# Values of two quads in one run from quad 44 on, in a fused cross-attention kernel

## The chip, the core and the metric

The kernel runs on one core of one Trainium2 chip. The metric is the time of one execution on the device in microseconds (us). Engines are named as in the profile: PE is TensorE (matmuls; PEld its weight loads), DVE VectorE, ACT ScalarE, POOL GpSimd, SP SyncE, whose queue issues nearly all transfers. Each engine works through its own list of instructions in order; semaphores tie the lists together.

## The reference

Eight batches of 256 tokens attend to 256 context rows each, with 32 heads of 32 columns. Keys and values are the context itself. All data are float32.

```python
x_ = (x - mu) * rsqrt(var + 1e-5) * ln_gamma + ln_beta      # (8, 256, 1024)
Q = split_heads(x_ @ Wq.T); K = V = split_heads(ctx)         # 32 heads x 32
scores = where(mask, einsum('bhsd,bhtd->bhst', Q, K) / sqrt(32), -inf)
probs = softmax(scores)
out = x + merge_heads(einsum('bhst,bhtd->bhsd', probs, V)) @ Wout.T
```

## The kernel before

**Quads and slots.** Four heads (128 columns) are a quad; eight batches of eight quads give 64. The main loop has a slot for each quad n, and the program's order is each engine's order (the schedule is manual). In slot n PE gets, in this order: the scores of quad n + 1 (line 493), output-projection steps of "place 0", the values of quad n - 2 (line 643), steps of "place 1", one eighth of a later batch's query projection (line 216, `pq`), and steps of "place 2". The softmax of quad n + 1 goes to the other engines in the same slot.

**Softmax** (`softmax_parts`), head by head of the quad: DVE adds the mask and takes the row minimum of the negated scores out of PSUM (line 531), ACT exponentiates and sums the row (535), DVE takes reciprocals (542), POOL scales (550), DVE transposes 32 x 32 blocks into the tile `pT` (556). ACT sets one half of `pT` aside (562), and SP's queue exchanges halves between partitions by four transfers (621, 625). Then PE can form the values. From quad 57 on the last transposes and the transfers (`tail`) are put off to the next quad's softmax. The first exponentials of a quad are followed, on ACT, by the copies of finished values: `copy_at` (line 656) takes the two PSUM banks of a quad, `pv` for r = 0 and 1, into the tile `at`, with one chunk for each quad and one tile for each half batch.

**Buffers.** `pT` has three buffers, tag `pv` two PSUM banks, the scores (`sc`) four, `pq` and `po` one each. The pool `xp` has two buffers, each of the size of a `pT`. They hold a batch's x and its transposed blocks `xe` in turn; the last batch's x is used up in slot 44, and its `xe` by transfers soon after. In slot 60 one buffer takes x again for the final sum (`x_again`).

**Projections.** The output projection of a batch is a 2 x 2 block product with seven products (Strassen-Winograd; `PRODUCTS`) of four steps each, one step for each chunk (quad) of the operand: A11 with quads 0 to 3, A12 with 4 to 7, then S2, S3, A22, S1, S4. The sums S1 to S4 are made by POOL (line 703). The 28 steps of batch b are spread over the slots 8(b + 1) to 8(b + 1) + 8 by a table with a triple for each slot, the number of steps at places 0, 1 and 2. The seventh batch has its own table, `ENDS`: its results are copied off the bank `po` by ACT (`copy_po`, line 745) and added by POOL. For the others DVE reads the bank: `take` (765) and `store` (769). A product that begins the bank anew, or adds to it, must wait for these readers. From slot 59 on a step of the last batch (`po_last`) stands at each slot's end. After the loop come the last batch's remaining products, `po_end` and `po_last`, between the values of quads 62 and 63.

**Order around the change.** The lists are written out by the loop; the transfers stand on SP's queue where a softmax issues them. A load of v for two quads is issued at the end of a softmax and waits until the buffer's last values are formed.

## Time and profile before

| | us |
|---|---|
| median of 3 executions (562.49 to 563.6) | 563.45 |
| the profiled execution, whole | 562.29 |
| its span (first to last instruction) | 560.5 |
| PE busy | 555.1 (99%) |
| DVE busy | 466.3 (83%) |
| ACT busy | 423.7 (76%) |
| POOL busy | 392.9 (70%) |

A row of a timeline gives the start, the time from the first start to the last end, the engine, the line, the tiles written and read, and how many instructions are merged; what stands in brackets is the engine's idle time before the row and what ended it. Runs on PE overlap at their ends, so what a run costs is the distance from its start to the next run's start. One matmul of float32 in the program is two in the profile: 32 rows of the lists below are x64 in a timeline. The slots 48 to 63 start with the scores at 416.50, 424.02, 432.34, 440.72, 449.96, 458.34, 466.73, 475.11, 483.49, 492.73, 499.33, 505.94, 512.54, 519.15 and 525.75, and slot 63, which has no scores, with values at 532.35.

### The profile page before, as it was taken

How to read it: one execution, taken by the hardware profiler on the slowest of the kernel's cores; microseconds unless marked ns; L12 is line 12 of the kernel's file. 1: busy time of each engine (PE TensorE's matmuls, PEld its weight loads, DVE VectorE, ACT ScalarE, POOL GpSimd, SP SyncE). 2: the span in 40 equal slices, each digit the busy share in tenths (PEclk: the TensorE clock that was granted, in tenths of full speed). 3: DMA queues.
4: the chain of work that ended last, by engine and by line, in shares of the span. 5: the costliest groups of instructions: out<-in, count | busy, mean ns of one | idle time of the engine just before them, and what ended most of it. 6: DMA issues, size and time to landing. Idle time of an engine off the chain costs nothing.

```text
span 560.5 us, 24339 instructions
## 1 busy us (share of the span) xinstructions
PE 555.1 (99%) x9334; PEld 357.0 (64%) x9334; DVE 466.3 (83%) x1716; ACT 423.7 (76%) x1464; POOL 392.9 (70%) x635
## 2 busy tenths in 40 slices
PE   8999999999999999999999999999999999999997
PEld 7666665767656767567765676566766766744443
DVE  5979889999998888988898888988888878879823
ACT  3699999998769867797777877778776876869920
POOL 1688887999797666867568666777648657448780
PEclk9999999999999999999999999999999999999999
DMA  8967657957678767877778767788667874536752
GB/s 305 397 188 209 184 150 235 319 179 223 207 253 246 246 183 223 259 204 232 217 232 233 207 186 233 221 233 239 176 166 249 244 228 130 149 91 182 209 169 76
DMA packets 47236, 119.30 MB, mean 213 GB/s; under 512 B 8976, under 2 KB 9744, under 8 KB 47120
## 3 DMA queue, kind: packets, MB, share of 16 engines
q1 hardware_dynamic: 46832, 117.48, 69.5%
q8 instruction: 74, 1.21, 1.0%
q14 instruction: 42, 0.34, 0.2%
q10 hardware_dynamic: 288, 0.27, 0.1%
HBM read 66.33 MB, written 11.53 MB: 139 GB/s over the span
## 4 chain that ended last, share of the span: by engine, by line
PE 98%; DVE 1%; DMA 1%; ACT 0%; POOL 0%; issue 0%; POOLq 0%
PE po_S L216 20%; PE pq_A L216 19%; PE pv L643 12%; PE sc L493 12%; PE po_A L216 11%; PE pq L216 10%; PE pq_S L216 7%; PE po_end L216 3%; PE po_last L216 1%; DMA x<-in_x_dram 1%; PE po_end_s L216 0%; PE px L280 0%; PE px L314 0%; ACT e L535 0%; DVE st L234 0%; DVE xnT L289 0%
## 5 line engine op out<-in xcount | busy, mean ns | idle before, releaser
L550 POOL TENSOR_SCALAR e<-e,rden 128x256 f32<-128x256 f32 x466 | 215.5, 479 | 124.2 <-DVE rden L542 121.7
L535 ACT ACTIVATE e<-e,mn 128x256 f32<-128x256 f32 x512 | 254.0, 501 | 43.6 <-DVE mn L531 43.1
L556 DVE STREAM_TRANSPOSE pT<-e 128x512 f32<-128x512 f32 x256 | 178.9, 703 | 36.6 <-POOL e L550 27.5
L531 DVE CUSTOM_DVE_ANT_0 e<-sc,mb 128x256 f32<-128x256 f32 x512 | 185.3, 416 | 23.8 <-PE sc L493 23.3
L562 ACT COPY pc<-pT 128x512 f32<-128x512 f32 x128 | 78.9, 616 | 52.2 <-DVE pT L556 34.5
L535 ACT ACTIVATION_READ_ACCUMULATOR e<-e,mn 128x1 f32 x512 | 98.2, 192 | 0.0
L493 PEld LDWEIGHTS sc<-k,qa 32*128 32x128 f32 x1024 | 46.1, 184 | 45.6 <-issue 22.4
L643 PE MATMUL pv<-pT,v 64*32 64x128 f32 x4096 | 74.2, 274 | 0.0
L493 PE MATMUL sc<-k,qa 32*128 32x256 f32 x1024 | 73.6, 400 | 0.2 <-ACT qa L301 0.2
L216 PE MATMUL po_S<-wo,at 128*64 128x512 f32 x304 | 73.5, 598 | 0.0
L643 PEld LDWEIGHTS pv<-pT,v 64*32 64x32 f32 x4096 | 57.1, 105 | 22.7 <-issue 9.6
L216 PE MATMUL po_A<-wo,at 128*64 128x512 f32 x256 | 58.6, 598 | 0.0
L216 PE MATMUL pq<-xnT,wq 128*64 128x256 f32 (+3 forms) x544 | 58.4, 369 | 0.0
L216 PEld LDWEIGHTS pq_A<-xnT,wq 128*64 128x64 f32 x832 | 46.3, 137 | 7.4 <-issue 6.3
L216 PE MATMUL po_S<-wo,s 128*64 128x512 f32 x208 | 49.5, 598 | 0.0
L216 PEld LDWEIGHTS pq<-xnT,wq 128*64 128x64 f32 x544 | 36.8, 136 | 18.9 <-issue 1.8
L216 PE MATMUL pq_A<-xnT,wq 128*64 128x128 f32 x832 | 47.6, 273 | 0.0
L542 DVE RECIPROCAL rden<-den 128x2 f32<-128x2 f32 x256 | 38.3, 150 | 5.8 <-ACT e L535 4.9
L531 DVE DVE_READ_ACCUMULATOR2_ANT mn<- 128x1 f32 x512 | 42.6, 83 | 0.0
L216 PEld LDWEIGHTS po_A<-wo,at 128*64 128x64 f32 x256 | 16.9, 136 | 30.0 <-issue 29.1
L216 PEld LDWEIGHTS po_S<-wo,at 128*64 128x64 f32 x304 | 19.3, 136 | 22.6 <-issue 22.6
L656 ACT COPY at<-pv 128x128 f32<-128x128 f32 x128 | 26.2, 254 | 8.7 <-PE pv L643 8.7
(99 smaller groups left out, 645.4 us busy)
## 6 DMA issues: line engine op xcount, KB each, us to landing
v<-in_kv_dram SPq DMA_DIRECT2D x32, 512.0 KB, 4.8
pT<-pT SPq DMA_DIRECT2D x128, 128.0 KB, 3.3
pT<-pc SPq DMA_DIRECT2D x128, 128.0 KB, 4.1
ring<-kept_T SPq DMA_DIRECT2D x20, 512.0 KB, 5.3
k<-in_kv_dram SPq DMA_DIRECT2D x32, 256.0 KB, 4.0
x<-in_x_dram SPq DMA_DIRECT2D x15, 512.0 KB, 6.6
r<-in_x_dram SPq DMA_DIRECT2D x28, 256.0 KB, 5.1
out_dram<-r SPq DMA_DIRECT2D x28, 256.0 KB, 2.6
```

The source lines that it names most:

```text
L216: nc.tensor.matmul(out[ts(w, P // 2)], stationary[:, ts(w, P // 2)], moving, **flags)
L493: nc.tensor.matmul(scs[n][j][:, s, :], qa[r, n % NQ, ts(s, P)], ks[n - n % 2][r, n % 2, :], start=True, stop=True,)
L531: nc.vector.tensor_tensor_reduce(out=e[:, s, :], in0=pss[j][:, s, :], in1=mbs[n // NQ], scale=1.0, scalar=NO_SCORE, op0=ALU.add, op1=ALU.m ...
L535: nc.scalar.activation(e[:, s, :], e[:, s, :], AF.Exp, bias=mn[:, s : s + 1], scale=-1.0, accum_out=den[:, s : s + 1],)
L542: nc.vector.reciprocal(rden, dens[j])
L550: engine.tensor_scalar(es[j][:, s, :], es[j][:, s, :], rden[:, s : s + 1], 1.0, ALU.mult, ALU.mult,)
L556: nc.vector.transpose(pT[:, :, :, j, :, :].rearrange("p a i s k -> p (a i) s k"), es[j].rearrange("p s (b t) -> p b s t", t=K),)
L562: nc.scalar.copy(pc[:, :, ts(j, 2)], pT[:, 1, :, ts(j, 2)])
L643: nc.tensor.matmul(pvs[n][r][j * HD : (j + 1) * HD], vs[n - n % 2][ts(r, 2 * K), i, ds(n % 2 * P + j * HD, HD)], pT[ts(r, 2 * K), :, i, j, ...
L656: nc.scalar.copy(ats[b, k][:, c, :, ts(r, 2), :], pv.rearrange("p a s k -> p s a k"))
```

## The change

From quad 44 to quad 61 the values of an even quad wait for the odd one behind it: in odd slots PE forms both in one run, in even slots none. Both quads share the two banks, at different columns. After the pair ACT copies four pieces instead of two. An even quad's `pT` is held a slot longer, so a fourth buffer is needed: every fourth quad from 47 on uses one tile out of the pool `xp`. The sixth batch (b = 5) gets a table of its own, since its last quads come in pairs; in slot 49 six steps follow the values instead of seven. The seventh batch's S2 sum is cut into halves instead of three chunks and one.

```diff
+        if n not in SPARE:
+            pTs[n] = ptp.tile([P, 2, NI, NH, NS, K], F32, tag="pT", name=f"pT_{n}")
+        else:
+            if n == SPARE[0]:
+                spare.append(xp.tile([P, 2, NI, NH, NS, K], F32, tag="x", name="pT_spare"))
+            pTs[n] = spare[0]
...
+    PAIRED = range(44, N - 2)
+    SPARE = range(47, N, 4)
+    def due(n):
+        if n - 2 not in PAIRED:
+            return (n - 2,)
+        return (n - 3, n - 2) if n % 2 else ()
...
-    def values(n):
-        pvs[n] = [
-            ps_v.tile([P, 2, NS, K], F32, tag="pv", name=f"pv_{n}_{r}") for r in range(2)
-        ]
+    def values(*quads):
+        if not quads:
+            return
+        banks = [
+            ps_v.tile([P, len(quads), 2, NS, K], F32, tag="pv", name=f"pv_{quads[0]}_{r}")
+            for r in range(2)
+        ]
+        for u, n in enumerate(quads):
+            pvs[n] = [bank[:, u] for bank in banks]
...
     STEPS = ((0, 0, 0), (0, 7, 0), (0, 1, 2), (0, 2, 2), (0, 2, 1), (0, 1, 2), (0, 0, 3), (0, 1, 2),
              (0, 2, 0))
+    STEPS_PAIRED = ((0, 0, 0), (0, 6, 0), (0, 2, 2), (0, 2, 1), (0, 3, 1), (0, 0, 3), (0, 0, 4),
+                    (0, 0, 1), (0, 3, 0))
...
         if n >= 2:
-            values(n - 2)
+            values(*due(n))
...
-            copy_at(n - 2)
+            for done in due(n):
+                copy_at(done)
...
-            sum_at(b, "S2", *((slice(NK - 1, NK),) if b == B - 2 else ()))
+            sum_at(b, "S2", *((slice(NK // 2, NK),) if b == B - 2 else ()))
...
-                sum_at(b, "S2", slice(0, NK - 1))
+                sum_at(b, "S2", slice(0, NK // 2))
```

Where this moves instructions is seen in three places. The first is PE's slot 54, between the scores of quad 55 and the S1 steps of the sixth batch (`po_5_S1`, which begins the bank again); `pq_7_A11` is the query product of the slot. Before, and then after the change:

```order
L493 MATMUL sc_55_3_8603<-k_54_8131,qa_143 128x256
L643 MATMUL pv_52_0_8612<-pT_52_8225,v_52_8286 32x128 [waits DMAHW4_49,DMAHW7_49,DMAHW2_49,Activation_49]
...
L216 MATMUL pq_7_A11_8350<-sx_145,ring_105 64x128 [waits DMAHW1_49,DVE_49,Pool_49]
...
L216 MATMUL po_5_S1_8744<-wo_149,s2_5_7981 64x512 [waits DVE_49,PE_49]
L216 MATMUL po_5_S1_8744<-wo_149,s2_5_7981 64x512 x5
...
L643 MATMUL pv_53_0_8764<-pT_53_8383,v_52_8286 32x128 [waits DMAHW6_49,DMAHW3_49,Activation_49]
```

```order
L493 MATMUL sc_55_3_8594<-k_54_8089,qa_143 128x256
L216 MATMUL pq_7_A11_8309<-sx_145,ring_105 64x128 [waits DMAHW1_49,DVE_49,Pool_49]
...
L216 MATMUL po_5_S1_8697<-wo_149,s2_5_7975 64x512 [waits DVE_49,PE_49]
L216 MATMUL po_5_S1_8697<-wo_149,s2_5_7975 64x512 x7
...
L665 MATMUL pv_52_0_8719<-pT_52_8215,v_52_8279 32x128 [waits DMAHW7_49,DMAHW4_49,Activation_49]
...
L665 MATMUL pv_52_0_8719<-pT_53_8342,v_52_8279 32x128 [waits DMAHW6_49,DMAHW3_49]
```

The values of quad 52 have left the slot and stand ahead of quad 53's in slot 55, in one bank; the steps, now eight rows instead of six, still wait for DVE.

The second is PE's slot 60, with the A22 steps of the seventh batch (`po_6_A11` is the bank's name, `at_6_1` the operand), which wait for ACT's `copy_po` of that bank. Before, and after:

```order
L493 MATMUL sc_61_3_9415<-k_60_9106,qa_143 128x256
L643 MATMUL pv_58_0_9424<-pT_58_9093,v_58_9226 32x128 [waits DMAHW3_49,DMAHW7_49,DMAHW1_49,Activation_49]
...
L216 MATMUL po_6_A11_9040<-wo_149,at_6_1_8687 64x512 [waits Activation_49]
L216 MATMUL po_6_A11_9040<-wo_149,at_6_1_8687 64x512 x7
L216 MATMUL po_last_9408<-wo_149,at_7_0_9232 64x512 x2
L493 MATMUL sc_62_0_9532<-k_62_9349,qa_143 128x256 [waits DMAHW7_49,DVE_49]
```

```order
L493 MATMUL sc_61_3_9398<-k_60_9090,qa_143 128x256
L216 MATMUL po_6_A11_8992<-wo_149,at_6_1_8826 64x512 [waits Activation_49]
L216 MATMUL po_6_A11_8992<-wo_149,at_6_1_8826 64x512 x7
L216 MATMUL po_last_9391<-wo_149,at_7_0_9335 64x512 x2
L493 MATMUL sc_62_0_9479<-k_62_9329,qa_143 128x256 [waits DMAHW7_49,DVE_49]
```

The values of quad 58 no longer stand between the scores and the waiting steps.

The third is the end of ACT's list: the softmax of quad 63 (its last exponentials, `e_63_3`), the half set aside (`pc`), `copy_po` (`ends`) and the copies of values. Before, and after:

```order
L656 COPY at_7_1_9715<-pv_60_0_9663 128x2x64 [waits PE_49]
L656 COPY at_7_1_9715<-pv_60_1_9664 128x2x64 [waits PE_49]
...
L535 ACTIVATE e_63_3_9736,den_63_3_9738<-e_63_3_9736,mn_63_3_9737 128x256 [waits DVE_49]
L562 COPY pc_63_9699<-pT_63_9698 128x4x128 [waits DMAHW7_49,DMAHW0_49,DVE_49]
L745 COPY ends_9334<-po_6_S1_9639 128x512 [waits PE_49]
L656 COPY at_7_1_9715<-pv_61_0_9771 128x2x64 [waits PE_49]
L656 COPY at_7_1_9715<-pv_61_1_9772 128x2x64 [waits PE_49]
```

```order
L541 ACTIVATE e_63_3_9679,den_63_3_9681<-e_63_3_9679,mn_63_3_9680 128x256 [waits DVE_49]
L568 COPY pc_63_9645<-pT_spare_7441 128x4x128 [waits DMAHW6_49,DMAHW5_49,DMAHW7_49,DMAHW0_49,DVE_49]
L769 COPY ends_9314<-po_6_S1_9620 128x512 [waits PE_49]
L678 COPY at_7_1_9781<-pv_60_0_9714 128x2x64 [waits PE_49]
L678 COPY at_7_1_9781<-pv_60_1_9715 128x2x64 [waits PE_49]
L678 COPY at_7_1_9781<-pv_60_0_9714 128x2x64
L678 COPY at_7_1_9781<-pv_60_1_9715 128x2x64
```

Quad 60's copies stood in the midst of quad 63's softmax, ahead of its exponentials for the second head; now they stand behind all of it, with quad 61's, and the second two of the four wait for nothing of their own: the first two wait for the whole pair. PE's first `po_end` matmuls read quad 60's chunk.

More of the change, by code (lines that the diff above doesn't have):

```diff
@@ L519, in softmax_parts @@
         pss = scs[n]
-        pT = pTs[n] = ptp.tile([P, 2, NI, NH, NS, K], F32, tag="pT", name=f"pT_{n}")
+        if n not in SPARE:
[4 more added lines that the diff above has]
+            pTs[n] = spare[0]
+        pT = pTs[n]
         pc = asp.tile([P, NI, NH, NS, K], F32, tag="pc", name=f"pc_{n}")
@@ L633, in softmax_parts @@
         yield
-    def values(n):
-        pvs[n] = [
-            ps_v.tile([P, 2, NS, K], F32, tag="pv", name=f"pv_{n}_{r}") for r in range(2)
-        ]
-        pT = pTs.pop(n)
-        for i in range(NI):
-            for j in range(NH):
-                for r in range(2):
-                    nc.tensor.matmul(
-                        pvs[n][r][j * HD : (j + 1) * HD],
-                        vs[n - n % 2][ts(r, 2 * K), i, ds(n % 2 * P + j * HD, HD)],
-                        pT[ts(r, 2 * K), :, i, j, :, :],
-                        start=(i == 0), stop=(i == NI - 1),
-                    )
+    PAIRED = range(44, N - 2)
+    SPARE = range(47, N, 4)
+    spare = []
+    def due(n):
[8 more added lines that the diff above has]
+            for r in range(2)
+        ]
+        for u, n in enumerate(quads):
+            pvs[n] = [bank[:, u] for bank in banks]
+            pT = pTs.pop(n)
+            for i in range(NI):
+                for j in range(NH):
+                    for r in range(2):
+                        nc.tensor.matmul(
+                            pvs[n][r][j * HD : (j + 1) * HD],
+                            vs[n - n % 2][ts(r, 2 * K), i, ds(n % 2 * P + j * HD, HD)],
+                            pT[ts(r, 2 * K), :, i, j, :, :],
+                            start=(i == 0), stop=(i == NI - 1),
+                        )
     def copy_at(n):
@@ L683, in steps_of @@
             return ENDS
-        return STEPS
+        return STEPS if b < PAIRED[0] // NQ else STEPS_PAIRED
     assert all(sum(map(sum, steps_of(b))) == len(PRODUCTS) * NK for b in range(B - 1))
```

## The prediction

> **What bounds the kernel now.** I read the page's parts 1 and 4 first, then the list of what TensorE (PE) waited for, then the timelines of slots 44 to 63.

> ```profile
> span 560.5 us, 24339 instructions
> PE 555.1 (99%) x9334; PEld 357.0 (64%) x9334; DVE 466.3 (83%) x1716; ACT 423.7 (76%) x1464; POOL 392.9 (70%) x635
> ...
> PE 98%; DVE 1%; DMA 1%; ACT 0%; POOL 0%; issue 0%; POOLq 0%
> ```

> The chain that ended last is TensorE nearly throughout. Its waits, in total, count and longest:

> ```profile
> PE busy L119 <- POOL ring masks.py:199: 1.3, 1, 1.3
> PE px L280 <- DVE ring L895: 1.0, 1, 1.0
> PE sc L493 <- ACT qa L301: 0.2, 1, 0.2
> ```

> All three lie before the first loop. From there TensorE never waits, so a microsecond off its list is one off the run, as long as the shorter list meets no wait. The question is how near the other engines are behind it in slots 46 to 63.

> **The change part by part.** *One run for two quads.* Start, length and count of the runs in slot 51:

> ```profile
> 440.72 1.15 PE L493 MATMUL sc<-k,qa 32*128 32x256 f32 x16
> 441.80 1.16 PE L643 MATMUL pv<-pT,v 64*32 64x128 f32 x64
> 442.88 1.94 PE L216 MATMUL po_S<-wo,s 128*64 128x512 f32 x8
> ```

> From start to start a run of values costs 442.88 - 441.80 = 1.08. The same run, cut off by a window after 24, 40 and 56 matmuls:

> ```profile
> 441.80 0.56 PE L643 MATMUL pv<-pT,v 64*32 64x128 f32 x24
> 441.80 0.83 PE L643 MATMUL pv<-pT,v 64*32 64x128 f32 x40
> 441.80 1.05 PE L643 MATMUL pv<-pT,v 64*32 64x128 f32 x56
> ```

> Sixteen more matmuls take 0.27 (40 against 24), the next sixteen 0.22, and the last eight 1.16 - 1.05 = 0.11, so 0.22 again. The rest of the 1.08 is the changeover from the scores and to the steps. A second quad right behind the first costs 4 x 0.22 = 0.88, at most 4 x 0.27 = 1.08. I take 0.88, the pace that the end of the run keeps, and a pair saves 0.20 (bounds 0 and 0.20). Does the even slot pay for its missing run? At the start there is one without values:

> ```profile
> 22.96 1.15 PE L493 MATMUL sc<-k,qa 32*128 32x256 f32 x16
> 24.04 3.70 PE L216 MATMUL pq<-xnT,wq 128*64 128x257 f32 x32
> ```

> Scores take 1.08 there too, as in slot 51 (441.80 - 440.72). So the whole 1.08 goes. Quads 44 to 61 are nine pairs: **-1.8**.

> *Steps dealt anew.* All 28 steps of the sixth batch stay, of one form, so TensorE pays nothing for the order. What moves is who must be done. I followed each hand-over of slots 46 to 57 through the timelines (banks, copies of the query products, ring loads, sums): where a step comes earlier by a slot's missing values its giver is mostly earlier too, and one is not. In slot 54 the bank of the products is read by VectorE (the store of line 769) before the S1 steps may begin it again:

> ```profile
> 466.73 1.15 PE L493 MATMUL sc<-k,qa 32*128 32x256 f32 x16
> 467.80 1.16 PE L643 MATMUL pv<-pT,v 64*32 64x128 f32 x64
> 468.89 3.71 PE L216 MATMUL pq_A<-sx,ring 128*64 128x128 f32 x64
> 472.43 2.75 PE L216 MATMUL po_S<-wo,s 128*64 128x512 f32 x12
> ...
> 467.89 0.42 DVE L531 CUSTOM_DVE_ANT_0 e<-sc,mb 128x256 f32<-128x256 f32 x1 [1.32 <-PE sc L493]
> ...
> 470.71 0.69 DVE L769 TENSOR_TENSOR r<-po_S,r 128x512 f32<-128x512 f32 x1
> ```

> VectorE starts with the scores, 1.16 behind the slot, and its read ends 471.40 - 466.73 = 4.67 into it. Without the values TensorE arrives after 1.07 + 3.54 = 4.61 instead of 5.70. With some 0.05 for the signal that is 0.1 of waiting; slot 46, same hand-over, the same. **+0.2** (bounds 0 and 0.6).

> *Sums in halves.* The S2 sum of the seventh batch is cut 2 + 2 chunks instead of 3 + 1. GpSimd then idles:

> ```profile
> 491.21 1.00 POOL L703 TENSOR_TENSOR s<-at,at 128x384 f32<-128x384 f32 x1
> 496.83 3.25 POOL L550 TENSOR_SCALAR e<-e,rden 128x256 f32<-128x256 f32 x7 [4.62 <-DVE rden L542]
> ```

> 4.62 idle covers it; uncovered it would be a chunk, 0.3. *The spare.* The buffer that quad 47 takes was last read by the blocks of x, and the first transpose of quad 47's probabilities is this far behind it:

> ```profile
> 391.43 1.21 DVE L323 STREAM_TRANSPOSE xe<-x 128x1024 f32<-128x1024 f32 x1
> ...
> 404.30 0.69 DVE L556 STREAM_TRANSPOSE pT<-e 128x512 f32<-128x512 f32 x1
> ```

> Both are VectorE's, 11.7 apart, so nothing waits: 0. The loads of v on SyncE's queue, which must not overtake the values that read the old v, are issued at a softmax's end, after the pair of the same slot: 0 too; uncovered, each would be late by the 0.9 that the pair ends later.

> *Four copies at a time on ScalarE.* In odd slots the copies of two quads (line 656) stand between the first and the second exponentials:

> ```profile
> 509.45 0.41 ACT L656 COPY at<-pv 128x128 f32<-128x128 f32 x2
> 509.76 0.51 ACT L535 ACTIVATE e<-e,mn 128x256 f32<-128x256 f32 x1
> ```

> Two occupy 0.31, so what is behind them comes 0.3 later: the exponentials, the reciprocals on VectorE that await them, GpSimd's scaling, the next transposes. A part of it is taken up where these wait for one another anyway; I take 0.2 (bounds 0 and 0.4, all of it and a little of the copies' own wait for the pair, which ends some 0.9 later than a single run). This costs nothing while VectorE has time. It has, up to slot 57, and then not:

> ```profile
> 493.89 0.42 DVE L531 CUSTOM_DVE_ANT_0 e<-sc,mb 128x256 f32<-128x256 f32 x1 [2.07 <-PE sc L493]
> 500.50 0.43 DVE L531 CUSTOM_DVE_ANT_0 e<-sc,mb 128x256 f32<-128x256 f32 x1 [0.18 <-PE sc L493]
> ...
> 526.91 0.42 DVE L531 CUSTOM_DVE_ANT_0 e<-sc,mb 128x256 f32<-128x256 f32 x1 [0.17 <-PE sc L493]
> ```

> From slot 58 on slots last 6.6 and VectorE's softmax nearly as long: it waits 0.17 to 0.18 for scores, where it waited 2.07. There the saved time is not passed on.

> *The last slots, step by step.* TensorE, then ScalarE:

> ```profile
> 512.54 1.15 PE L493 MATMUL sc<-k,qa 32*128 32x256 f32 x16
> 513.62 1.16 PE L643 MATMUL pv<-pT,v 64*32 64x128 f32 x64
> 514.70 3.65 PE L216 MATMUL po_A<-wo,at 128*64 128x512 f32 x16
> ...
> 519.15 1.15 PE L493 MATMUL sc<-k,qa 32*128 32x256 f32 x16
> ...
> 525.75 1.15 PE L493 MATMUL sc<-k,qa 32*128 32x256 f32 x16
> ...
> 532.35 1.16 PE L643 MATMUL pv<-pT,v 64*32 64x128 f32 x64
> 533.44 3.65 PE L216 MATMUL po_end<-wo,at 128*64 128x512 f32 x16
> ...
> 513.49 0.58 ACT L745 COPY ends<-po_A 128x512 f32<-128x512 f32 x1
> ...
> 533.55 0.43 ACT L656 COPY at<-pv 128x128 f32<-128x128 f32 x2
> ```

> Slot 58 starts six pairs earlier, less the two small waits: -1.2 + 0.2 = -1.0. Its scores set VectorE off 1.0 earlier, and ScalarE's copy of the bank (line 745) in slot 59, behind four copies, ends at 514.07 - 1.0 + 0.2 = 513.27. TensorE needs it in slot 60 for its A22 steps. Slots 58 and 59 now last 6.6 - 1.08 and 6.6 + 0.88, so slot 60 starts at 511.3 and, with no values between, TensorE stands at the steps at 512.4: **+0.9** of waiting, to 513.3. Slot 61 starts 4.45 later (519.15 - 514.70), at 517.8, slot 62 7.48 after that, at 525.25: 0.5 earlier than before. So VectorE's last softmax, and all of ScalarE behind it, is 0.5 earlier. Slot 63 starts at 530.8 and its pair is through at 532.7. Now comes po_end, whose first matmuls need quad 60. Before, it was copied a slot earlier. Now its two copies stand where those of quad 61 stood, at 533.55 - 0.5 = 533.05, last 0.43, and let TensorE go on at 533.5: **+0.8**. Before it was there at 533.44. Behind that stands the list as it was. What is late next is quad 62's transposed half, ended here (issues and us to landing):

> ```profile
> L625 SPq DMA_DIRECT2D pT<-pc x2: 507/507/507, 531.9 to 532.8; - x2
> ...
> DMA to landing us min/median/max: 3.7/3.7/3.7
> ```

> 532.8 + 3.7 = 536.5 less 0.5 is 536.0; its values come 3.58 after po_end, at 537.1. It waits for nothing.

> The sum: -1.8 + 0.2 + 0.9 + 0.8 = **+0.1**, a span of 560.6. The profiled execution took 562.29 for its 560.5, so 562.4; the median of the three runs, 563.45, lies 1.16 above it, so 563.5.

> **The rivals.** *The gain arrives* (chance 0.20). ScalarE and VectorE move forward with TensorE, and only the last hand-over remains. For it: 76% and 83% busy on the page, and the 2.07 of slot 57. Against: 0.17 and 0.18 after it. The least at slot 63 is a signal, two copies and the last matmuls' end, 0.05 + 0.43 + 0.07 = 0.55, so -1.8 + 0.55 = -1.25: 562.2. [...]

> *The second quad costs a full run* (0.10), the slower side: its first matmuls wait on semaphores of four transfers, in mid-run, and the sixteens go on at 0.27. Then slot 58 starts 0.2 later than before, ScalarE's copy ends at 514.07 + 0.4, slot 61 starts at 518.95, slot 62 at 526.63, 0.9 later, and po_end at 534.9: +1.5, 565.0. Against it: 0.22 for the last sixteen above, at an unbroken pace. It decides from a saving of under 0.05 a pair.

> *The spare does not free anything* (0.05): quad 47's buffer waits, or SyncE's transfers. Some tenths, 563.9.

> **How the numbers follow.** The forecast has 0.65. By its own bounds (copies that delay nothing and no wait in 46 and 54: the same steps give -0.3; the upper ends +0.6) it holds 563.1 to 564.1. The range takes in the gain that arrives, and half of the slower side: 562.0 to 564.6. About 0.2%, 1.1 us, is what a measurement can tell from no change. Faster by more: 0.18 of the first rival and 0.02 of the forecast, 0.20. Slower by more: 0.10, 0.05 of the forecast and 0.01: 0.16. The same: 0.64.

> **What would show it.** Values in odd slots in one run of 128, next start after 1.96; none in even ones. Waits of TensorE that are not there now: 0.1 on VectorE at S1 in slots 46 and 54, near 0.9 on ScalarE before the steps of slot 60, near 0.8 on ScalarE at po_end in slot 63. If the third and fourth are missing, the gain arrived; if the run takes over 2.1, the pair saves nothing. I am wrong if a hand-over in slots 47 to 57 waits that I took for free, or if VectorE's softmax in the last slots is quicker than 6.4.

## The result, and the profile after

| | before | after |
|---|---|---|
| median of 6 executions | 563.14 us | 569.38 us |
| lowest, highest | 562.49, 563.6 | 565.44, 572.53 |
| profiled execution | 562.29 | 572.06 |
| its span | 560.5 | 570.3 |

After stands to before as 1.011, with a 95% interval of 1.008 to 1.0136: slower, by about 6 us, where no change was forecast. Also new is the spread, 7 us instead of 1 (the kernel before, in the larger sets run beside the experiments, spread over 2 to 4).

The page after, first and fourth part (busy time and instructions of each engine; the chain that ended last, by engine):

```profile
span 570.3 us, 24323 instructions
PE 556.6 (98%) x9334; PEld 359.3 (63%) x9334; DVE 465.9 (82%) x1716; ACT 424.1 (74%) x1464; POOL 392.8 (69%) x635
...
PE 91%; DMA 2%; DVE 2%; issue 2%; ACT 1%; POOL 1%; ACTq 0%; DVEq 0%; SPq 0%; POOLq 0%
```

The same instructions and nearly the same busy time, but the chain has pieces called "issue": time in which the engine waited for nothing that the profile shows. TensorE's list of waits (total, count, longest) says where:

```profile
PE po_A L216 <- issue: 2.5, 1, 2.5
PE pv L665 <- issue: 1.7, 2, 1.3
PE px L280 <- DVE ring L919: 1.5, 1, 1.5
PE pq_A L216 <- issue: 1.3, 1, 1.3
PE busy L119 <- POOL ring masks.py:199: 1.3, 1, 1.3
PE pv L665 <- DMA pT<-pc: 1.1, 1, 1.1
PE po_A L216 <- ACT ends L769: 0.8, 1, 0.8
PE po_end L216 <- ACT at L678: 0.4, 1, 0.4
```

Three of these lines name no engine. They are four gaps. TensorE's timeline around them, in slots 49, 51, 53 and 55, and then a pair without one, in slot 57:

```profile
425.82 1.16 PE L665 MATMUL pv<-pT,v 64*32 64x128 f32 x64
426.71 1.21 PE L665 MATMUL pv<-pT_spare,v 64*32 64x128 f32 x64
427.85 1.93 PE L216 MATMUL po_A<-wo,at 128*64 128x512 f32 x7
432.26 4.08 PE L216 MATMUL po_A<-wo,at 128*64 128x512 f32 x17 [2.48 <-issue]
436.27 1.15 PE L493 MATMUL sc<-k,qa 32*128 32x256 f32 x16
...
445.50 2.07 PE L665 MATMUL pv<-pT,v 64*32 64x128 f32 x125
448.89 0.41 PE L665 MATMUL pv<-pT,v 64*32 64x128 f32 x3 [1.31 <-issue]
449.22 1.94 PE L216 MATMUL po_S<-wo,s 128*64 128x512 f32 x8
...
466.71 3.71 PE L216 MATMUL pq_A<-sx,wq 128*64 128x128 f32 x62
471.76 0.32 PE L216 MATMUL pq_A<-sx,wq 128*64 128x128 f32 x1 [1.35 <-issue]
...
474.70 1.15 PE L493 MATMUL sc<-k,qa 32*128 32x256 f32 x16
...
484.18 2.09 PE L665 MATMUL pv<-pT,v 64*32 64x128 f32 x127
486.63 0.29 PE L665 MATMUL pv<-pT,v 64*32 64x128 f32 x1 [0.36 <-issue]
486.85 3.71 PE L216 MATMUL pq_A<-xnT,wq 128*64 128x128 f32 x64
...
501.44 1.16 PE L665 MATMUL pv<-pT,v 64*32 64x128 f32 x64
502.34 1.21 PE L665 MATMUL pv<-pT_spare,v 64*32 64x128 f32 x64
503.48 4.51 PE L216 MATMUL po_A<-wo,at 128*64 128x512 f32 x20
```

The gap of slot 51 lies inside a values run, three matmuls before its end; that of slot 49 lies in the middle of one step, and the list gives no releaser for any of them. What the gaps cost, as the stretch from start to start less the same work without a gap: slot 51, 449.22 - 445.50 = 3.72 against 503.48 - 501.44 = 2.04, so 1.7; slot 55, 486.85 - 484.18 = 2.67, so 0.6. In slot 49 the 24 steps' matmuls take 436.27 - 427.85 = 8.42; before, 28 took

```profile
426.18 6.23 PE L216 MATMUL po_A<-wo,at 128*64 128x512 f32 x28
432.34 0.93 PE L493 MATMUL sc<-k,qa 32*128 32x256 f32 x12
```

6.16, which for 24 is 5.3: 3.1. In slot 53 query product and steps take 474.70 - 466.71 = 7.99, before (slot 54, the same 64 and 12) 475.11 - 468.89 = 6.22: 1.8. Together **7.2 us**, more than the 5.5 that the list shows as idle: the list counts from the end of the last matmul's record, and in an unbroken run the next matmul starts well before that end (one of the values takes 0.27 by its record, and sixteen take 0.22).

The other parts of the 9.8 us between the spans: 1.5 lie before quad 44, mostly one values run that waited 1.1 for its transfer in slot 18 (the line `pv <- DMA pT<-pc`; waits like it, of 0.3 to 2.1, come up in most of the runs below, in one of the kernel before with a longer list too); 1.2 are the two waits on ScalarE; 0.4 is VectorE's bank in slots 46 and 54 (below); nine pairs give back 9 x (2 x 1.085 - 2.04) = 1.2. That makes 9.1; 0.7 I did not place.

**What the gaps have in common.** I numbered TensorE's instructions from 0 (matmuls, weight loads and the few semaphore instructions between them, in order of their starts in the trace) and looked at the first one behind each gap. The third part of the page has a queue of its own for instructions. Its rows before the change (packets, MB, share of 16 engines; after it there are the same 74):

```profile
q1 hardware_dynamic: 46832, 117.48, 69.5%
q8 instruction: 74, 1.21, 1.0%
```

74 packets, 1.21 MB: 16,384 bytes each. TensorE has 18,668 matmuls and weight loads, and 18,901 instructions with those of its sequencer, nearly all for semaphores, which the page's counts leave out: 255 for a packet. From the trace's packets and starts (us; "block" is the time from TensorE's entry into the 256 instructions to the start of their last; "behind" the time from the packet's end to the next instruction; "gap" the time from the start of the block's last instruction to the next one's):

```
slot  first after gap   rest mod 256  block  packet starts  took  behind  gap
 49        14785            193        3.33   entry + 3.85  1.08   1.48   3.07
 51        15297            193        2.13   entry + 1.49  0.96   1.26   1.58
 53        16065            193        4.63   entry + 3.80  1.07   1.38   1.62
 55        16577            193        1.82   entry + 0.13  0.93   1.39   0.63
```

The rest is the remainder of the number divided by 256. All four lie at the same place of a block of 256, its border, and each time TensorE goes on 1.3 to 1.5 after the end of a packet of queue q8. In the kernel before the shortest block lasts 4.79; here a pair, 256 instructions in 2.04, leaves 1.8 to 4.6.

### The profile page after: what moved, and what is told of

Its sections match the earlier page's. It is cut to its first block, busy times and chain, and to the rows that moved or that the text cites. A ratio compares the mean times of both kernels' runs of the same rounds, so it can differ in the third digit from the quotient of the medians.

```text
span 570.3 us, 24323 instructions
## 1 busy us (share of the span) xinstructions
PE 556.6 (98%) x9334; PEld 359.3 (63%) x9334; DVE 465.9 (82%) x1716; ACT 424.1 (74%) x1464; POOL 392.8 (69%) x635
## 3 DMA queue, kind: packets, MB, share of 16 engines
q8 instruction: 74, 1.21, 1.0%
## 4 chain that ended last, share of the span: by engine, by line
PE 91%; DMA 2%; DVE 2%; issue 2%; ACT 1%; POOL 1%; ACTq 0%; DVEq 0%; SPq 0%; POOLq 0%
PE po_S L216 20%; PE pq_A L216 19%; PE sc L493 11%; PE pv L665 11%; PE pq L216 10%; PE po_A L216 8%; PE pq_S L216 7%; PE po_end L216 3%; POOL e L556 1%; DMA pT<-pc 1%; PE po_last L216 1%; DMA pT<-pT 1%; DMA x<-in_x_dram 1%; ACT e L541 1%; DVE e L537 1%
## 5 line engine op out<-in xcount | busy, mean ns | idle before, releaser
L556 POOL TENSOR_SCALAR e<-e,rden 128x256 f32<-128x256 f32 x466 | 215.4, 479 | 132.7 <-DVE rden L548 130.4
L562 DVE STREAM_TRANSPOSE pT<-e 128x512 f32<-128x512 f32 x236 | 164.8, 703 | 32.6 <-POOL e L556 25.6
L568 ACT COPY pc<-pT 128x512 f32<-128x512 f32 x118 | 72.6, 617 | 47.3 <-DVE pT L562 30.7
L493 PEld LDWEIGHTS sc<-k,qa 32*128 32x128 f32 x1024 | 45.9, 184 | 45.9 <-issue 27.2
L493 PE MATMUL sc<-k,qa 32*128 32x256 f32 x1024 | 73.7, 401 | 0.2 <-ACT qa L301 0.2
L216 PE MATMUL po_S<-wo,at 128*64 128x512 f32 x304 | 73.5, 598 | 0.0
L665 PE MATMUL pv<-pT,v 64*32 64x128 f32 x3776 | 68.7, 274 | 2.8 <-issue 1.7
L665 PEld LDWEIGHTS pv<-pT,v 64*32 64x32 f32 x3776 | 53.5, 105 | 22.5 <-issue 11.2
L216 PE MATMUL po_A<-wo,at 128*64 128x512 f32 x256 | 59.3, 599 | 3.3 <-issue 2.5
L216 PE MATMUL pq<-xnT,wq 128*64 128x256 f32 (+3 forms) x544 | 58.4, 369 | 0.0
L216 PEld LDWEIGHTS pq_A<-xnT,wq 128*64 128x64 f32 x832 | 46.2, 137 | 7.0 <-issue 5.1
L216 PE MATMUL po_S<-wo,s 128*64 128x512 f32 x208 | 49.4, 599 | 0.1
L216 PEld LDWEIGHTS pq<-xnT,wq 128*64 128x64 f32 x544 | 36.9, 136 | 18.8 <-issue 1.8
L216 PE MATMUL pq_A<-xnT,wq 128*64 128x128 f32 x832 | 47.7, 273 | 0.0
L216 PEld LDWEIGHTS po_A<-wo,at 128*64 128x64 f32 x256 | 16.9, 136 | 34.4 <-issue 32.0
L216 PEld LDWEIGHTS po_S<-wo,at 128*64 128x64 f32 x304 | 20.1, 136 | 23.0 <-issue 22.0
```

What stands on the lines that cost most here:

```text
L216: nc.tensor.matmul(out[ts(w, P // 2)], stationary[:, ts(w, P // 2)], moving, **flags)
L493: nc.tensor.matmul(scs[n][j][:, s, :], qa[r, n % NQ, ts(s, P)], ks[n - n % 2][r, n % 2, :], start=True, stop=True,)
L556: engine.tensor_scalar(es[j][:, s, :], es[j][:, s, :], rden[:, s : s + 1], 1.0, ALU.mult, ALU.mult,)
L562: nc.vector.transpose(pT[:, :, :, j, :, :].rearrange("p a i s k -> p (a i) s k"), es[j].rearrange("p s (b t) -> p b s t", t=K),)
L568: nc.scalar.copy(pc[:, :, ts(j, 2)], pT[:, 1, :, ts(j, 2)])
L665: nc.tensor.matmul(pvs[n][r][j * HD : (j + 1) * HD], vs[n - n % 2][ts(r, 2 * K), i, ds(n % 2 * P + j * HD, HD)], pT[ts(r, 2 * K), :, i, j, ...
```

## The experiments

The kernel before, run beside them, had medians of 563.2 to 563.5.

**The same work, with the borders moved.** More small matmuls at the start; nothing else.

```diff
-    for _ in range(26):
+    for _ in range(16):
         nc.tensor.transpose(busy, ident, ident)
+    for _ in range(53):
+        nc.tensor.matmul(busy[:K, :K], ident[:K, :K], ident[:K, :K], start=True, stop=True)
```

> The changed kernel with 192 more TensorE instructions ahead of the first real work: 16 instead of 26 of the 128 x 128 transposes that stand at the start (20 instructions less, a matmul and its weight load each), and 53 matmuls of 32 x 32 (212 more). Nothing behind is changed, so each instruction keeps its neighbours and waits, but lies 192 places further in TensorE's list. Theory F (fetch): TensorE's list arrives in transfers of 16 KB, 256 instructions each, one block ahead; a pair of quads is 256 instructions in 2.04 us, and where it fills a block, the next block is not there in time. With the borders moved by 192, worked out from the starts in the trace of the change less its four gaps, no block of slots 46 to 63 is shorter than 3.5 us, where the four that ended in a gap had 3.3, 2.1, 4.6 and 1.8: the gaps together fall from 7.3 us to 0 to 1.5, and the time from 569.4 to 563 to 565. Theory H (hand-over): the pair's own surroundings (four copies, banks, the fourth buffer, the steps dealt anew) make TensorE stand; then the gaps stay at the same matmuls and the time stays at 569.4, give or take the spread of 565.4 to 572.5. The small matmuls cost 0 to 1.5 at the start.

With 37 for 53:

> The same with 128 more instructions (16 transposes, 37 small matmuls). Theory F: the gaps leave slots 49, 51 and 55 and come up where a pair now fills a block: by the starts in the trace of the change less its gaps the short blocks are then 2.2 us at the pair of slot 47, 2.1 at that of slot 53, 2.5 at that of slot 57 and 2.7 at that of slot 61; the one of slot 53 is the surest, as large transfers are under way there. Together 3 to 9 us, so 565 to 572: the time need not fall, the places must move. Theory H: gaps at the matmuls of slots 49, 51, 53 and 55 as before, 569.4.

And the first edit made in the kernel before:

> The kernel before with the same 192 instructions more at the start as in the first shifted kernel: the control for what they cost by themselves. In the trace of that one the first scores came 4.6 us later than in the kernel before. Theory F (the list of TensorE comes late at a border of 256 instructions when a pair fills a block): the kernel before has no short block wherever the borders lie, so it pays the 4.6 and little more, 567.5 to 569, and of the 571.65 of the shifted change some 3 to 4 are gaps still. Rival: the extra instructions cost all of the 8.2 by which the shifted change lies above the kernel before, then 571 to 572 here too, and the shifted change had no gaps to speak of in most executions.

Measured: 192 places 571.65 us; 128 places 574.05; the kernel before with 192 places 569.42. The gaps of the two profiled executions of the changed kernel, first with 192, then with 128 (slots 51 and 55; 47, 51 and 53):

```profile
452.52 2.62 PE L218 MATMUL pq_S<-xnT,wq 128*64 128x128 f32 x44 [1.16 <-issue]
487.22 2.07 PE L218 MATMUL pq_A<-xnT,wq 128*64 128x128 f32 x33 [0.29 <-issue]
```

```profile
413.85 0.40 PE L667 MATMUL pv<-pT,v 64*32 64x128 f32 x2 [1.64 <-issue]
452.30 0.88 PE L218 MATMUL pq_S<-xnT,wq 128*64 128x128 f32 x12 [1.01 <-issue]
468.48 0.51 PE L667 MATMUL pv<-pT_spare,v 64*32 64x128 f32 x2 [3.18 <-issue]
```

The gaps have left their matmuls, and each new one is again at a rest of 193: 15553 and 16833; 14273, 15553 and 16065. H says that they stay, so it falls for the gaps. F named slots 47 and 53 for the 128 places, and both came; 57 and 61, which it named too, had none, and the one in slot 51 it had not named. For 192 places it gave 563 to 565 and at most 1.5 more: far too low, for two reasons. The new start costs 6.0 by itself, as the control shows (569.42 - 563.4; the first scores come 4.6 later in the trace of the shifted change than in that of the kernel before, and 6.0 later in the control's); and 571.65 lies 2.2 above the control, where the unmoved change lies 6.2 above its own. So by the medians the borders' place decided about two thirds of the loss, not all of it: in the trace of the 192 places two blocks were still late, of 4.4 and 3.3. The share is rough, since there are four executions of each, 569.2 to 575.6 and 568.3 to 572.1; in the traces the gaps, from start to start, fall from 6.9 to 2.0. For the 128 places F gave 565 to 572 and for the control 567.5 to 569; both came out above it.

**The one run undone, all else kept.**

```diff
-        if n >= 2:
-            values(*due(n))
+        if n - 2 in PAIRED:
+            values(n - 2 - n % 2, n - 1 - n % 2, part=n % 2)
+        elif n >= 2:
+            values(n - 2)
```

(`part` forms one quad of the pair in its own slot, in the same shared banks.)

> Of the change only the one run is undone: the even quad's values stand in the even slot again, the odd quad's in the odd one. Kept are the shared banks, the four copies at a time behind the odd quad, the fourth buffer, the steps dealt anew and the sums in halves. Theory F: no block of 256 instructions is run in under 4.5 us again, so no gap with nothing to wait for; what is left is the wait of 0.4 at po_end for the copies of quad 60 and perhaps some tenths for the four copies: 563.0 to 564.3. Theory H: what makes TensorE stand is still there, 567 to 570.

Measured: 564.98 us, 1.0026 of before (1.0015 to 1.0037). No gap in slots 46 to 63. Of 6.2 us that the change cost, taking the one run apart removes 4.7; so the run is what counts, and the copies, banks, buffer, steps and sums are worth 1.5 at most. With these 1.5 it lies 0.7 above F's upper end; 0.4 of them is the wait at po_end, the rest I can't assign. One gap was there, far from the change, where nothing is paired:

```profile
183.86 0.44 PE L674 MATMUL pv<-pT,v 64*32 64x128 f32 x15
184.74 0.95 PE L674 MATMUL pv<-pT,v 64*32 64x128 f32 x49 [0.43 <-issue]
```

Its number is 5825, rest 193, and its packet started 7.0 after the entry, into a block of 8.75: this late block was a long one.

**The steps and the halves alone.**

```diff
-    PAIRED = range(44, N - 2)
-    SPARE = range(47, N, 4)
+    PAIRED = range(0)
+    SPARE = range(0)
```

(and the table's choice written as `b < 5`)

> No pair at all, and so no fourth buffer and two copies at a time; kept are the sixth batch's steps dealt anew and the seventh's S2 sum in halves. Theory F: the same as before, 563.0 to 564.0. Theory H, in the form that hand-overs of the steps dealt anew in slots 46 to 57 make TensorE stand: 565 or more, with waits on ScalarE, VectorE or GpSimd in those slots.

Measured: 564.19 us, 1.001 of before (0.9991 to 1.0029): not to be told from no change (0.2 above F's figure), and TensorE waits for no engine in those slots.

**Tail and head apart.** `PAIRED = range(56, N - 2)` with the old steps and sums; then `PAIRED = range(44, 56)` with the new ones.

> Pairs only for quads 56 to 61 (slots 59, 61 and 63), with the steps and sums of the kernel before. The trace of the change has no gap at a border in these slots, but the two waits on ScalarE, 0.8 in slot 60 and 0.4 at po_end. Theory F: 0.8 + 0.4 less three times 0.13 that a pair saved there (2.04 for a pair, two runs at 1.085), +0.8: 563.9 to 564.7. Rival (the last slots carry most of the loss): 566 or more.

> Pairs only for quads 44 to 55 (slots 47 to 57), from quad 56 on single runs as before; the steps dealt anew, the halves and the fourth buffer are kept. Borders and transfers are those of the change. Theory F: gaps at the borders in slots 49, 51, 53 and 55 as in the change, without the waits of slots 60 and 63: 567.5 to 569.5. Rival (the last slots): 563 to 564.

Measured: the tail 564.44 us, 1.0017 (1.0008 to 1.0027); the head 568.91, 1.0091 (1.0053 to 1.0129). Both times as F said. TensorE's only new waits for an engine in the tail are the two that the prediction had named, 0.80 and 0.37 (there are three for transfers too, 1.1, 0.4 and 0.3, like the one of slot 18 above):

```profile
516.35 3.65 PE L216 MATMUL po_A<-wo,at 128*64 128x512 f32 x16 [0.80 <-ACT ends L769]
536.39 3.81 PE L216 MATMUL po_end<-wo,at 128*64 128x512 f32 x16 [0.37 <-ACT at L678]
```

The head's profiled execution was its quickest, 565.83, and shows how the same list can cost less: its gaps stand at 14785, 15297 and 16577, the numbers of the change itself, but are 0.5 to 0.9 long from start to start, and slot 53, which F named too, has none: the packet of slot 49 started 1.64 after the entry and not 3.85. That is the spread of the change in small.

**Fewer transfers beside it.**

```diff
-            if b > SPLIT:
+            if SPLIT < b < B - 1:
                 for half, slot in enumerate(slots):
                     rings[slot].append(partial(load_ring, name, half))
```

> The changed kernel without the six transfers of 512 KB that bring the last batch's weight sums into the ring (slots 47 to 52); its queries are formed from what stood there, so the output of the last batch is another. TensorE's list, its blocks and their borders are the same. Theory F: in the trace of the change the fetches in slots 49 and 53 began 3.9 and 3.8 us after TensorE had entered the block, behind such transfers; without them some 1 us as in most others, so the gaps there fall from 3.2 and 1.8 to 0 to 0.5, those in slots 51 and 55 (1.7 and 0.6) stay: 569.4 falls to 564.5 to 566.5. If fetches don't queue behind data, and for theory H, nothing changes: 568 to 570.

Measured: 566.55 us, 1.0056 (1.003 to 1.0082), just above F's figure and below H's. Slots 49, 51 and 55 have gaps at the same numbers as in the change, 0.8, 0.8 and 1.0 long from start to start; slot 53 has none. So in slots 49 and 53 the gaps shrank or went, as F said, though 0.8 is above its 0.5; slots 51 and 55, which it held fixed, changed as well. The executions of the two kernels overlap (564.9 to 570.9 here), so this run alone would not show it. All traces together point the same way: 763 blocks of eleven kernels (without the first and last few of each), sorted by how busy the 16 DMA engines were with data in the 2 us after TensorE had entered the block:

```
share busy    blocks   packet starts after the entry: median   longest
under 0.3        70                  0.2                          1.3
0.3 to 0.6      153                  0.4                          4.3
0.6 to 0.8      132                  1.0                          4.1
0.8 to 0.95     196                  1.1                          6.5
over 0.95       212                  1.9                          7.0
```

The median start goes from 0.2 us after the entry, where the DMA engines were under 0.3 busy with data, to 1.9, where they were over 0.95 busy. That the packet stands in a queue behind the data is my reading of this; no trace shows the queue itself. In slot 49 of the change the engines were 94 to 95% busy ahead of the gap and in it (columns: the window, its length, then busy time of PE, PEld, DVE, ACT, POOL, the granted clock, the DMA share, GB/s):

```profile
424.00:429.00 5.00, 5.00 (x166) 3.61 (x163) 4.74 (x19) 2.71 (x11) 4.43 (x7) 1.00 0.94 283
429.20:432.30 3.10, 0.62 (x5) 0.04 (x2) 2.38 (x9) 2.95 (x13) 2.64 (x6) 1.00 0.95 296
```

The 74 packets of 16,384 bytes for 18,901 instructions and the gaps at one rest of 256 agree with blocks of 256. Taken in order with the borders, the packets start about when TensorE enters a block (a median of 0.7 to 1.2 later by kernel; 0.74 before the change, 0.87 after it), and the gaps stand at that block's end. In the kernel before, with no block shorter than 4.79, there was no gap; the four blocks of the change that ended in one lasted 1.82 to 4.63, the one above 8.75.

**The burst by itself, in the kernel before.** Values of eight odd quads formed twice, far from the change.

```diff
-        for i in range(NI):
+        twice = 2 if 22 <= n < 38 and n % 2 else 1
+        for i in [i for _ in range(twice) for i in range(NI)]:
             for j in range(NH):
```

> The kernel before, without pairs and far from the place of the change: the values of eight odd quads, 23 to 37, are formed twice in a row (the same matmuls again, into the same banks, with the same result), so 256 instructions stand back to back in eight slots, 25 to 39. What the second forming costs by itself is 0.949 as in a pair (2.036 less 1.087): 8 x 0.949 = 7.6. Theory F: by the starts in the trace of before with those runs put in, four of the blocks of 256 become shorter than 2.5 us, in slots 25 (2.1), 35, 37 (2.5 both) and 39 (2.3); in the runs so far a block whose fetch began at once still took 3.1 us, so each of the four has a gap of 0.6 or more, up to 3 or 4 where the fetch queues behind data: 563.4 + 7.6 + 3 to 8 = 574 to 579, with every gap at an instruction whose number is 193 over a multiple of 256. Rival (the gaps of the change come from what else it does around quads 44 to 55): no gaps, 571.0 give or take 0.7.

Measured: 578.55 us (571.26 to 578.92). The added matmuls alone would make 571, and one of the four executions took no more; the other three lie at 578.5 to 578.9. There the rest is gaps and what follows them: in the profiled execution, 578.61, gaps of 4.3 and 1.3 from start to start and 1.7 of clock (last section). The gaps stand in slots 25 and 37; slot 35's burst has none:

```profile
225.19 2.01 PE L644 MATMUL pv<-pT,v 64*32 64x128 f32 x126
231.20 0.38 PE L644 MATMUL pv<-pT,v 64*32 64x128 f32 x2 [3.99 <-issue]
231.50 7.92 PE L216 MATMUL po_A<-wo,at 128*64 128x512 f32 x28
...
319.39 2.10 PE L644 MATMUL pv<-pT,v 64*32 64x128 f32 x128
321.42 1.94 PE L216 MATMUL po_S<-wo,s 128*64 128x512 f32 x8
...
337.96 1.95 PE L644 MATMUL pv<-pT,v 64*32 64x128 f32 x118
340.95 0.43 PE L644 MATMUL pv<-pT,v 64*32 64x128 f32 x10 [1.05 <-issue]
```

Numbers 7617 and 11969, rest 193 both. No pair of quads, no fourth buffer, no new steps: 256 instructions back to back were enough in slots 25 and 37, and not in slots 35 and 39. Two of the four gaps that F named did not come, so my floor of 3.1 for a block was wrong; slot 55 of the change, 0.13 + 0.93 + 1.39 = 2.45, had already shown less. In slot 35 the packet started 0.12 after the entry and took 0.92, and TensorE went on 1.38 behind its end without a gap, just in time for a block of 2.43; in slot 39 it started 0.97 before TensorE entered the block. So there the packet was under way before TensorE's matmuls reached the block; why it was early stays open.

Over all runs 18 gaps of this kind were seen, every one at a rest of 193, and behind every one TensorE went on 1.25 to 1.60 after the packet's end. From this I estimate what a block of 256 needed in these traces: the packet's delay, its own time (a median of 1.10 before the change and 1.15 after it), and about 1.4 more; the gap is what the block's own work fell short of that. Worked out with 1.4 for all 807 blocks between two borders in the eleven traces, this need exceeds the block by more than 0.3 in the 18 and in no other, and gives each gap to within 0.2. Being short was not enough: of the 17 blocks under 3 us ten had a gap, and in the other seven the packet started at once (two) or 1.0 to 3.1 before TensorE entered the block (five, that of slot 59 in the change among them).

## Why the prediction was wrong, point by point

- **The step that failed** is the second half of the reading of the bound: "From there TensorE never waits, so a microsecond off its list is one off the run, as long as the shorter list meets no wait." I then looked for waits at every engine, queue and bank, and not at the list itself. The second quad was priced by the pace at which matmuls run (0.22 per sixteen), with the instructions taken as given. The missing term is 7.2 in the profiled execution; taking the runs apart again is worth 4.7 in the medians (6.2 over before against 1.5). The page of before had the row for it, unread: queue q8, 74 packets, 1.21 MB, against 2 x 9334 instructions. With the pair's 256 in 2 us that asks for a packet in 2 us, and the DMA engines were 69.5% busy with data.
- **A pair saves 0.20:** 0.13. The pair takes 2.04 and not 1.96, because its second quad costs 0.95 and not 0.88: its first sixteen matmuls take 0.26 and its third sixteen 0.25, where I took 0.22 for all. (By its matmuls' starts a single run keeps 0.22 from the ninth matmul on; the 0.27 read there comes from ends.) Nine pairs give 1.2, not 1.8.
- **VectorE's bank in slots 46 and 54, +0.1 each:** 0.2 each. Query product to steps, slot 46 after:

```profile
402.28 3.71 PE L216 MATMUL pq_A<-sx,ring 128*64 128x128 f32 x64
406.02 2.79 PE L216 MATMUL po_S<-wo,s 128*64 128x512 f32 x12
```

  3.74 from start to start, where the same took 3.54 in slot 54 before. Slot 54 after the change has 3.75. Right place; the forecast was half of it.
- **ScalarE before the steps of slot 60, +0.9:** 0.8, and 0.7 to 0.8 in all five kernels that keep that pair; with the runs taken apart and in the head alone it is not there. Right.
- **ScalarE at po_end in slot 63, +0.8:** 0.4 wherever quads 60 and 61 share their copies. Right place, twice too large.
- **The fourth buffer, the sums in halves, the queue of SyncE, at nothing:** no wait on any of them appears.
- **The rival on the slower side** (a second quad costs a full run, through semaphores in mid-run) had the sign and nearly the place, but not the cause: where the list is there, the pair runs through in 2.04 with no break.
- **What would prove me wrong** was to be a hand-over in slots 47 to 57. The time was lost in those slots, but no engine handed anything over late. The range, 562.0 to 564.6, was built from the pairs' saving and hand-overs alone, so it could not reach 569.

With the terms at their measured sizes, the change without its gaps is -1.2 + 0.4 + 0.8 + 0.4 = +0.4. So there is no version of it in these runs that beats the kernel before: pairs in the head alone would gain about 0.4 (six pairs, less the bank's 0.4) if no block were late, less than can be measured.

## What to carry to other kernels

Ask of a busy engine not only what it waits for but how fast it uses up its list: the page's instruction queue against the engine's count gives instructions per packet, 255 here. Of the 17 blocks that used one up in under 3 us, ten had a gap behind them, and the packets started later where data filled the DMA engines (a median of 1.9 against 0.2). The dense blocks here were small matmuls packed back to back; a run of values among slower matmuls cost 1.085, where the second of a pair cost 0.95, but in the four kernels here without such pairs no block took under 4.6 us, and one block in all was late. The sign was "issue" gaps at one rest of the instruction number (193 of 256, all 18), which moved to other matmuls when the list was shifted by 128 or 192.

## What the runs showed of the hardware that was not expected

The granted clock of TensorE fell behind three long stands. After the burst's gap of 4.0 the 28 rows of po_A took 7.92 instead of 6.23, and the window shows a granted clock of 0.66, back at 1.00 in the next:

```profile
226.00:231.00 5.00, 1.20 (x88) 0.94 (x71) 2.42 (x15) 1.52 (x6) 2.17 (x3) 1.00 0.90 296
231.00:236.00 5.00, 4.80 (x16) 1.55 (x17) 2.63 (x6) 3.22 (x13) 2.75 (x6) 0.66 0.70 213
236.00:240.00 4.00, 4.00 (x28) 1.48 (x28) 2.24 (x5) 1.62 (x3) 4.00 (x5) 1.00 0.08 18
```

The same came after the gap of 3.2 with the list moved by 128 (0.62 in the 4 us behind it) and, in the kernel before with 192 more instructions, after a wait of 2.1 for a transfer (0.62). After the gap of 2.5 in slot 49 of the change it did not (1.00). The traces also hold the times at which the granted clock changed. In all three cases it was 0.5 for 3.41 us, so the stand cost 1.7 more than itself. In all eleven traces a stretch at one clock, up to the end of the work, lasts a whole multiple of 3.413 (157.0, 225.3 and 457.4 before the three drops, or 46, 66 and 134 times), so I cut the runs into windows of that length. In the window just ahead of a drop TensorE stood for 2.1, 2.4 and 3.2; up to the end of its work it stood for at most 1.8 in any other. The gap of 2.5 in slot 49 fell across two windows, 1.3 in one and 1.2 in the next. The ends of the traces go the same way: where TensorE's last matmuls left 2.1 to 3.0 of their window empty (five traces) the clock fell at once, where they left 0.2 to 1.4 (six) one window later. So in these traces the drops went with how much of one window the stand filled, 2.1 to 3.2 against 1.8 at most, and not with its length alone; what sets the clock they do not show. One more drop doesn't fit standing time: in the run moved by 128 it came at 7.8 us, behind a window of 32 x 32 matmuls with 0.2 of standing.

Little of the change's 6 us came this way: the mean granted clock of its six executions was 1.0 in four of them and 0.997 in two, and 0.003 of 568 us is one loss of 1.7.
